# The 42-column remainder of a feed-forward: from half-array tiles to the full shape of TensorE

## The chip, the cores and the metric

The kernel runs on one core of a Trainium2 chip (trn2). The metric is the device time of one execution in microseconds (us); lower is better. The times shown are those of several executions of the same program, and one further execution was recorded by the hardware profiler.

## The reference

The program computes `x = x + ffn(cond(x, t))` for 32 sequences of 256 tokens with 256 channels, in float32. `cond` is a gated scan over the tokens (512 inner channels, a state of 16). `ffn` has two layers; each is a windowed attention with 8 heads and then a gated feed-forward. Only the feed-forward is touched here:

```python
HID = int(DIM * 4 * 2 / 3)          # 682
...
h = shift_token(x)
mu = h.mean(-1, keepdims=True)
var = h.var(-1, keepdims=True)
h = (h - mu) / jnp.sqrt(var + 1e-05) * lg + lb
h = h @ w1 + b1                     # 256 -> 2 x 682
a, g = jnp.split(h, 2, axis=-1)
h = a * jax.nn.gelu(g, approximate=False)
x = x + h @ w2 + b2                 # 682 -> 256
```

682 is five blocks of 128 and a remainder of 42 (`MREM`). The last of the six blocks is what this case is about.

## The kernel before

**Tiling and order.** The 32 sequences go through the scan in four groups of eight (`GB`). The scan of group g+1 runs beside attention and feed-forward of group g; the feed-forward of the last group runs with no scan beside it. For attention and feed-forward the unit of work is one sequence in one layer, of which there are 32 x 2 = 64. Each unit has a list of stages, eight to a step (`ST = 8`), written out by hand in `attend`, `feed` and `fetch`; at every stage a share of the scan's steps is put out as well (`scan_to`). The instructions of each engine run in the order in which the program puts them out. Matrix products are in float32, and each appears in the trace as two matmul records with their two weight loads (two passes).

**The feed-forward of a unit.** `normalise`, `apply` and `spread` make `self.h`, the normalised channels-by-tokens block (2 x 128 channels by 256 tokens). `widen(m)` (L1313, matmuls at L1326) multiplies it with block m of `w1`, once for the linear half `pa` and once for the gate half `pg`, each over two blocks of channels (`KM = 2`); ScalarE then writes Gelu(pg + bias) to a tile `ag` (L1334). `product(m)` (L1337, instruction at L1342) multiplies `ag` by `pa` + bias on VectorE. `narrow(d)` (L1348, matmuls at L1354), for each of the two output halves d, sums over the six blocks `ag[m]` with `w2` into `po_f`, and VectorE adds the residual (L1365). In `feed`, for unit n, `widen(m)` stands at stage 4 + m and `product(m)` at stage 5 + m of step n+2, and `narrow(d)` at stage 3 + d of step n+3. A remainder's `widen(5)` is therefore at stage 1 of step n+3.

**The remainder as it is now.** In `widen`, the linear half (42 columns) goes to partitions 0 to 41 of a PSUM bank and the gate half (42 columns) to partitions 64 to 105. These are two tiles of the array, 64 columns wide, and the loop alternates between them. `product` writes its result twice, to partitions 64 to 105 and 0 to 41 of `ag`. `narrow` uses the lower copy for d = 0 and the upper one for d = 1, each as a matmul over 42 rows, in a tile of 64 rows. The 42 rows of `w2` for the upper copy are loaded by an extra transfer (L954) to partitions 64 on.

**Buffers.** `ag` has seven buffers and takes six of them for each unit. All PSUM tiles share one ring of eight banks (`ps_w`). Weights are single buffers, reloaded for each group and layer by SyncE's queue (`load_weights`, L939). In memory, `w2` is padded with zero rows to 6 x 128; `w1` is not padded, its 1364 columns are the linear half and then the gate half.

Of the kernel before, what the change touches and what calls it, by code (L numbers as in the profile page):

```python
# [10 lines left out]
FP = mybir.dt.float32  # L11
# [3 lines left out]
ALU = mybir.AluOpType  # L15
# [4 lines left out]
P = 128  # L20
S = 256
DM = 256
KM = DM // P
# [14 lines left out]
DH = 64  # L38
W = 128
NW = S // W  # L40
HID = 682
MCH = [(o, min(P, HID - o)) for o in range(0, HID, P)]
MREM = MCH[-1][1]
# [30 lines left out]
def kernel(  # L74
# [29 lines left out]
    nc = tc.nc  # L104
# [58 lines left out]
    for j in range(NJ):  # L163
# [18 lines left out]
        out=mask_t[:, 0:W], in_=mask_t[:, 0:W], compare_op=ALU.is_ge, fill=MASKED_LOW,  # L182
# [3 lines left out]
        out=mask_t[:, W : 2 * W], in_=mask_t[:, W : 2 * W], compare_op=ALU.is_ge,  # L186
# [22 lines left out]
    b1_sb = const.tile([P, L, 2, len(MCH)], FP, tag="b1_sb", name="b1_sb")  # L209
# [7 lines left out]
    for i in range(2):  # L217
        t = const.tile([P, NI * (P + GB)], FP, tag=f"ly{i}", name=f"ly{i}")
# [3 lines left out]
    def program(ctx, exact):  # L222
        rpool = ctx.enter_context(tc.tile_pool(name="res", bufs=1, reuse_waits="tile"))
# [7 lines left out]
        aw = ctx.enter_context(tc.tile_pool(name="aw", bufs=3, reuse_waits="tile"))  # L231
        ps_w = ctx.enter_context(tc.tile_pool(name="psw", bufs=8, space=PSUM, reuse_waits="tile"))

        def bank(pool, tag, name):
            return pool.tile([P, DI], FP, tag=tag, name=name)
# [694 lines left out]

        ys, res, wt, projected = {}, {}, {}, {}

        def load_res(g, b):
            t = rpool.tile([P, KM, 1 + S], FP, tag=f"res{b}", name=f"res{b}")
            nc.gpsimd.memset(t[:, :, 0:1], 0.0)
            nc.sync.dma_start(out=t[:, :, 1:], in_=ys[g][:, :, b, :])
            res[b] = t

        def load_weights(l, kind, i=0):  # L939
            shape, srcs = {  # L940
                "qkv": lambda: ([P, KM, DI], [wqkv[:, l, :, i * DI : (i + 1) * DI]]),
                "wo": lambda: ([P, NC_, DM], [wo[:, l]]),
                "w1": lambda: (
                    [P, KM, 2, MCH[i][1]],
                    [w1[:, l, :, x * HID + MCH[i][0] :][:, :, 0 : MCH[i][1]] for x in range(2)],
                ),
                "w2": lambda: ([P, len(MCH), DM], [w2[:, l]]),
            }[kind]()
            t = wpool.tile(shape, FP, tag=f"{kind}{i}", name=f"{kind}{i}")
            for x, src in enumerate(srcs):  # L950
                nc.sync.dma_start(out=t[:, :, x] if len(srcs) > 1 else t, in_=src)
            if kind == "w2":
                last = len(MCH) - 1
                nc.sync.dma_start(out=t[DH : DH + MREM, last], in_=w2[0:MREM, l, last])  # L954
            wt[kind, i] = t

        WEIGHTS = [("qkv", 2), ("qkv", 0), ("qkv", 1), ("wo", 0)]
# [67 lines left out]
        if exact:  # L1025
# [4 lines left out]
                out=mask[:, 0:W], in_=mask[:, 0:W], compare_op=ALU.is_ge, fill=MASKED,  # L1030
# [3 lines left out]
                out=mask[:, W : 2 * W], in_=mask[:, W : 2 * W], compare_op=ALU.is_ge, fill=MASKED,  # L1034
# [218 lines left out]
        class FeedForward:  # L1253
# [59 lines left out]
            def widen(self, m):  # L1313

                l, n = self.l, MCH[m][1]
                ps = bank(ps_w, "w", "pa")
                pa = ps[0:n, 0:S]
                if n == P:
                    pg, b1g = ps[:, S:], b1_sb[:, l, 1, m : m + 1]
                    order = [(x, k) for x in (1, 0) for k in range(KM)]  # L1320
                else:

                    pg, b1g = ps[DH : DH + n, 0:S], b1g_sb[DH : DH + n, l : l + 1]
                    order = [(x, k) for k in range(KM) for x in (1, 0)]
                for x, k in order:
                    nc.tensor.matmul(  # L1326
                        pg if x else pa,
                        wt["w1", m][:, k, x],
                        self.h[:, k],
                        start=(k == 0),  # L1330
                        stop=(k == KM - 1),
                    )
                ag = aw.tile([P, S], FP, tag="ag", name="ag", bufs=7)
                nc.scalar.activation(ag[0:n], pg, AF.Gelu, bias=b1g)  # L1334
                self.pa[m] = pa, ag

            def product(self, m):  # L1337
                l, n = self.l, MCH[m][1]
                pa, ag = self.pa.pop(m)

                for r in (0,) if n == P else (DH, 0):
                    nc.vector.scalar_tensor_tensor(  # L1342
                        ag[r : r + n], pa, b1_sb[0:n, l, 0, m : m + 1], ag[0:n],
                        ALU.add, ALU.mult,
                    )
                self.ag[m] = ag

            def narrow(self, d):  # L1348
                if d == 0:
                    self.po = bank(ps_w, "w", "po_f").rearrange("p (d t) -> p d t", d=KM)  # L1350
                for m, (_, n) in enumerate(MCH):

                    r0 = 0 if n == P else d * DH
                    nc.tensor.matmul(  # L1354
                        self.po[:, d],
                        wt["w2", 0][r0 : r0 + n, m, d * P : (d + 1) * P],
                        self.ag[m][r0 : r0 + n],
                        start=(m == 0),
                        stop=(m == len(MCH) - 1),
                    )  # L1360
                l, last = self.l, self.l == L - 1
                if d == 0 and last:
                    self.fo = ap_.tile([P, KM, S], FP, tag="swp", name="fo", bufs=3)
                rv = res[self.b][:, d, 1:]
                nc.vector.scalar_tensor_tensor(  # L1365
                    self.fo[:, d] if last else rv,
                    self.po[:, d], b2_sb[:, l, d : d + 1], rv, ALU.add, ALU.add,
                )
                if last and d == KM - 1:
                    b = self.g * GB + self.b  # L1370
                    xs = ap_.tile([P, KM, S], FP, tag="rot", name="xs", bufs=4)
                    nc.sync.dma_start(out=xs, in_=xT[:, :, b, :])
                    nc.gpsimd.tensor_add(self.fo, self.fo, xs)
                    nc.sync.dma_start(out=outT[:, :, b, :], in_=self.fo)

        NM = len(MCH)
        if exact:
            for g in range(NG):
                for _ in scan_slots([g]):
                    pass  # L1380
                for b in range(GB):
                    load_res(g, b)
                for l in range(L):
                    for kind, i in WEIGHTS:
                        load_weights(l, kind, i)
                    for _ in attention(l):
                        pass
                    for b in range(GB):
                        ff = FeedForward(g, l, b)
                        ff.normalise()  # L1390
                        ff.apply()
                        ff.spread()
                        for m in range(NM):
                            ff.widen(m)
                            ff.product(m)
                        for d in range(KM):
                            ff.narrow(d)
            return
# [43 lines left out]
        def fetch(n, g, l, b):  # L1442

            if b == GB - 1 and (g, l) != (NG - 1, L - 1):
                nl = (l + 1) % L
                for i, a in ((5, 2), (6, 0), (6, 1)):
                    stage(n - 1, i, load_weights, nl, "qkv", a)
                stage(n + 2, 0, load_weights, nl, "wo")
                for m in range(NM):
                    stage(n + 2, 6 + m, load_weights, nl, "w1", m)  # L1450
                stage(n + 3, 6, load_weights, nl, "w2")
            if l == L - 1 and g < NG - 1:
                stage(n + 6, 2, load_res, g + 1, b)
# [22 lines left out]
        for b in range(GB):  # L1476
            load_res(0, b)
# [7 lines left out]
        for t in range(max(stages) + 1):  # L1485
# [3 lines left out]
            g, r = divmod(t + 1 + group - reload, group)  # L1489
# [10 lines left out]
    with tc.If(fits > 0) as which:  # L1500
        with ExitStack() as es:
            program(es, False)
    with which.Else():
        with ExitStack() as es:
            program(es, True)
# [108 lines left out]
```

## Time and profile before

| what | value |
|---|---|
| median of 3 runs | 3692.19 us (3688.66 to 3693.34) |
| span of the profiled execution (first to last instruction; the profile gives no other time for it) | 3693.9 us |
| mean granted TensorE clock | 0.988 |
| busy TensorE / its weight loads | 3580.5 / 2234.3 us |
| busy VectorE / ScalarE / GpSimd | 2714.2 / 2163.0 / 1812.1 us |
| matmul records at L1326 (`widen`) / L1354 (`narrow`) | 3072 / 1536 |
| instructions at L1342 (`product`) | 448, of which 128 on 42 partitions, 475 ns each |

How to read the lines that follow: in the tables of groups, a line gives the line of the code, the engine (PE is TensorE, PEld its weight loads, DVE VectorE, ACT ScalarE, POOL GpSimd, SP SyncE), the operation, output<-inputs, for matmuls rows*columns of the stationary block and the moving operand, the count, and then busy time, mean duration and idle time before it. A line of the timeline gives the start in us, the time from there to the end of the last instruction merged into it, and the instructions. The ends of matmuls are modelled, and the records of consecutive matmuls overlap; their starts are what to compare. A line of the waits gives who waited for whom, us in total, times and the longest.

### The profile page before, as it was taken

Reading aid. Unit: us, or ns where it says so; the run is one execution under the profiler, and the core shown is the slowest. Engines: PE = TensorE matmul, PEld = TensorE weight load, DVE = VectorE, ACT = ScalarE, POOL = GpSimd, SP = SyncE. Lnnn points to the kernel's source line nnn. Section 1 sums busy time; section 2 is a strip of 40 time slices with the busy share of each in tenths; the row PEclk is TensorE's granted clock in tenths of the full one; section 3 lists DMA queues with packets and bytes.
Section 4 is the critical chain, followed back from the end, with each engine's and each line's share of the span. In section 5 each row is a group of like instructions: output and inputs, shape, how many; then the busy total and the mean of one; then the engine's idle time right before and its main releaser. Section 6 shows DMA issues by size and latency. Waiting matters only on the chain.

```text
span 3693.9 us, 56916 instructions
## 1 busy us (share of the span) xinstructions
PE 3580.5 (97%) x19804; PEld 2234.3 (60%) x19804; DVE 2714.2 (73%) x5177; ACT 2163.0 (59%) x3689; POOL 1812.1 (49%) x1745
## 2 busy tenths in 40 slices
PE   7999989999999999999999999999999999999999
PEld 4444335666566566666666666666666666666666
DVE  5888889878787777877787778877777445455553
ACT  3666656666666666666666666666666444444442
POOL 4433366445455455545455556544554444444551
PEclk9999999999999999999999999999999999999999
DMA  7877655544454555444454555544453212011101
GB/s 196 209 201 206 185 164 148 134 110 135 124 139 119 140 141 145 131 112 124 119 138 124 135 145 138 134 111 130 111 134 114 59 35 59 12 30 39 30 27 36
DMA packets 469213, 435.80 MB, mean 118 GB/s; under 512 B 228835, under 2 KB 308532, under 8 KB 468788
## 3 DMA queue, kind: packets, MB, share of 16 engines
q1 hardware_dynamic: 384466, 420.05, 42.2%
q10 hardware_dynamic: 84450, 12.01, 2.1%
q8 instruction: 160, 2.62, 0.3%
q14 instruction: 137, 1.12, 0.1%
HBM read 383.70 MB, written 46.66 MB: 117 GB/s over the span
## 4 chain that ended last, share of the span: by engine, by line
PE 67%; DVE 15%; DMA 5%; POOL 5%; ACT 3%; issue 3%; SPq 0%; ACTq 0%; DVEq 0%; POOLq 0%
PE ps_qkv L965 13%; PE pa L1326 13%; PE po_f L1354 8%; DVE h L706 6%; PE y L718 5%; PE ps_wo L1015 4%; PE sc L1174 4%; DMA xrep<-xnd 4%; PE ov L1223 3%; PE ps_out L796 3%; PE ps_in L398 2%; PE tr_qk L1004 2%; DVE acc L488 2%; PE rs L1204 2%; ACT xrep L696 2%
## 5 line engine op out<-in xcount | busy, mean ns | idle before, releaser
L706 DVE CUSTOM_DVE_ANT_0 h<-h,xrep,lim 128x512 f32<-128x512 f32 x1024 | 947.3, 925 | 232.2 <-ACT xrep L696 197.5
L696 ACT ACTIVATE xrep<-xrep,beta 128x512 f32<-128x512 f32 x960 | 672.8, 719 | 336.1 <-DMA xrep<-xnd 239.0
L965 PE MATMUL ps_qkv<-qkv,res 128*128 128x512 f32 x1536 | 724.7, 607 | 19.2 <-DVE ag L1342 8.3
L1326 PE MATMUL pa<-hT,w 128*128 128x256 f32 (+1 forms) x3072 | 690.4, 387 | 1.6 <-ACT hT L1305 1.3
L1326 PEld LDWEIGHTS pa<-hT,w 128*128 128x128 f32 (+1 forms) x3072 | 493.8, 178 | 186.6 <-issue 77.8
L989 POOL TENSOR_TENSOR rot<-rot,swp 128x512 f32<-128x512 f32 x256 | 335.4, 1310 | 482.4 <-DVE swp L986 353.2
L965 PEld LDWEIGHTS ps_qkv<-qkv,res 128*128 128x128 f32 x1536 | 278.0, 191 | 328.9 <-issue 250.0
L997 POOL TENSOR_TENSOR rn<-ss,neg_half 128x8 f32<-128x8 f32 x256 | 459.2, 1794 | 15.6 <-DVE ss L995 5.4
L1354 PE MATMUL po_f<-ag,w 128*128 128x256 f32 (+1 forms) x1536 | 388.5, 394 | 11.5 <-DVE ag L1342 7.6
L1342 DVE SCALAR_TENSOR_TENSOR ag<-pa,b_sb,ag 128x256 f32<-128x256 f32 (+1 forms) x448 | 213.1, 476 | 234.4 <-ACT ag L1334 231.8
L718 PE MATMUL y<-h,ly 128*32 128x512 f32 x2048 | 357.1, 614 | 10.7 <-DVE h L706 7.9
L1279 POOL TENSOR_TENSOR rstd<-ve,neg_half 128x2 f32<-128x2 f32 x64 | 46.4, 724 | 614.8 <-DVE ve L1277 596.9
L1354 PEld LDWEIGHTS po_f<-ag,w 128*128 128x128 f32 (+1 forms) x1536 | 273.4, 189 | 119.5 <-issue 47.3
L998 POOL TENSOR_TENSOR rot<-rot,rn 128x512 f32<-128x512 f32 x256 | 291.0, 1137 | 20.1
L978 ACT ACTIVATE sq<-ps_qkv 128x512 f32<-128x512 f32 x256 | 151.9, 596 | 229.3 <-PE ps_qkv L965 181.0
L1334 ACT ACTIVATE ag<-pa,b_sb 128x256 f32<-128x256 f32 x320 | 150.4, 470 | 206.1 <-PE pa L1326 203.6
L488 DVE SCALAR_TENSOR_TENSOR acc<-xr,wc_sb,acc 128x256 f32<-128x256 f32 x384 | 192.7, 524 | 55.7 <-POOL acc L477 55.1
L1015 PE MATMUL ps_wo<-oT,wo 128*128 128x256 f32 x1024 | 231.7, 379 | 0.3 <-ACT ag L1334 0.2
L981 DVE TENSOR_TENSOR rot<-ps_qkv,rc_sb 128x512 f32<-128x512 f32 x256 | 174.8, 683 | 73.4 <-ACT sq L978 72.3
L1174 PE MATMUL sc<-qT,kT 64*128 64x128 f32 (+1 forms) x2048 | 221.3, 345 | 0.0
L1183 ACT ACTIVATE pT<-sc 128x512 f32<-128x512 f32 x384 | 208.6, 596 | 15.2 <-PE sc L1174 13.2
L1015 PEld LDWEIGHTS ps_wo<-oT,wo 128*128 128x128 f32 x1024 | 194.3, 190 | 28.2 <-ACT ag L1334 1.0
(153 smaller groups left out, 5493.7 us busy)
## 6 DMA issues: line engine op xcount, KB each, us to landing
xrep<-xnd SPq DMA_DIRECT2D x960, 256.0 KB
rb<-inv SPq DMA_DIRECT2D x128, 256.0 KB
xnd<-xn SPq DMA_DIRECT2D x64, 256.0 KB
qkv<-in_wqkv_dram SPq DMA_DIRECT2D x24, 512.0 KB
ahead<-xs_a SPq DMA_DIRECT2D x48, 256.0 KB
xp<-ahead SPq DMA_DIRECT2D x48, 256.0 KB
xd<-xnd SPq DMA_DIRECT2D x192, 64.0 KB
w<-in_w_dram SPq DMA_DIRECT2D x80, 128.0 KB
```

Source lines behind the costliest of these rows:

```text
L488: nc.vector.scalar_tensor_tensor(acc, xr[:, :, k : k + CH], wc_sb[:, ch, k : k + 1], acc, ALU.mult, ALU.add,)
L696: scaled = nc.scalar.activation(bx, ck[c].pop(("bx", t), bx), AF.Copy, scale=ck[c]["beta"][:, t : t + 1])
L706: nc.vector._custom_dve(TENSOR_ADD_SAT, out=h_new, in0=state["h"], in1=bx, s0=ck[c]["lim"][:, 0, t : t + 1], s1=ck[c]["lim"][:, 1, t : t + 1],
L718: nc.tensor.matmul(ck[c]["y", hb][32 * q : 32 * q + 32, :], ly[hb % 2][:, 32 * t : 32 * t + 32], ck[c].pop(("h", hb * TB + t)), start=(i = ...
L965: nc.tensor.matmul(ps, res[b][:, k, t0 : t0 + W], wt["qkv", a][:, k], start=(k == 0), stop=(k == KM - 1),)
L989: nc.gpsimd.tensor_add(rot, rot, swp)
L997: nc.gpsimd.tensor_tensor(rn, ss, neg_half, ALU.pow)
L998: nc.gpsimd.tensor_mul(rot, rot, bc(rn, 2, DH))
L1015: nc.tensor.matmul(po[:, d], wt["wo", 0][:, c, d * P : (d + 1) * P], oT[:, c, :], start=(c == 0), stop=(c == NC_ - 1),)
L1174: nc.tensor.matmul(banks[r][:, i, :], kT[rows, i0 + i, kw * W : (kw + 1) * W], qT[rows, i0 + i, kw * W :], start=self.apart, stop=self.apa ...
L1326: nc.tensor.matmul(pg if x else pa, wt["w1", m][:, k, x], self.h[:, k], start=(k == 0), stop=(k == KM - 1),)
L1354: nc.tensor.matmul(self.po[:, d], wt["w2", 0][r0 : r0 + n, m, d * P : (d + 1) * P], self.ag[m][r0 : r0 + n], start=(m == 0), stop=(m == le ...
```

## The change

The two halves of the remainder become one stationary block of 106 columns: 64 columns that begin with the 42 linear ones (the other 22 are the first columns of the gate half of `w1`, whose results are not read), and then the 42 gate columns. One chain of two matmuls takes the place of two chains; the results lie on the same partitions as before. The remainder's `ag` becomes a tile of its own, `ag_rem`, allocated once and set to zero once by GpSimd; Gelu and product write its first 42 partitions, product only once. `narrow` runs over all 128 rows for every block: rows 42 to 127 are zero in `ag_rem` and in `w2`. The extra transfer for `w2` goes, the first half of the remainder's `w1` transfer has 64 columns and not 42, and `ag` has six buffers.

```diff
+        ag_rem = rpool.tile([P, S], FP, tag="ag_rem", name="ag_rem")
+        nc.gpsimd.memset(ag_rem, 0.0)
...
                 "w1": lambda: (
-                    [P, KM, 2, MCH[i][1]],
-                    [w1[:, l, :, x * HID + MCH[i][0] :][:, :, 0 : MCH[i][1]] for x in range(2)],
+                    [P, KM, 2, P] if MCH[i][1] == P else [P, KM, 1, DH + MREM],
+                    [w1[:, l, :, x * HID + MCH[i][0] :] for x in range(2)],
                 ),
...
-            for x, src in enumerate(srcs):
-                nc.sync.dma_start(out=t[:, :, x] if len(srcs) > 1 else t, in_=src)
-            if kind == "w2":
-                last = len(MCH) - 1
-                nc.sync.dma_start(out=t[DH : DH + MREM, last], in_=w2[0:MREM, l, last])
+            if kind == "w1":
+
+                dst = [t[:, :, 0], t[:, :, 1]] if MCH[i][1] == P else [
+                    t[:, :, 0, 0:DH], t[:, :, 0, DH:]
+                ]
+            else:
+                dst = [t]
+            for out, src in zip(dst, srcs):
+                nc.sync.dma_start(out=out, in_=src[:, :, 0 : out.shape[-1]])
...
                 if n == P:
                     pg, b1g = ps[:, S:], b1_sb[:, l, 1, m : m + 1]
-                    order = [(x, k) for x in (1, 0) for k in range(KM)]
+                    dst, xs = (pa, pg), (1, 0)
                 else:
 
                     pg, b1g = ps[DH : DH + n, 0:S], b1g_sb[DH : DH + n, l : l + 1]
-                    order = [(x, k) for k in range(KM) for x in (1, 0)]
-                for x, k in order:
-                    nc.tensor.matmul(
-                        pg if x else pa,
-                        wt["w1", m][:, k, x],
-                        self.h[:, k],
-                        start=(k == 0),
-                        stop=(k == KM - 1),
-                    )
-                ag = aw.tile([P, S], FP, tag="ag", name="ag", bufs=7)
+                    dst, xs = (ps[0 : DH + n, 0:S],), (0,)
+                for x in xs:
+                    for k in range(KM):
+                        nc.tensor.matmul(
+                            dst[x],
+                            wt["w1", m][:, k, x],
+                            self.h[:, k],
+                            start=(k == 0),
+                            stop=(k == KM - 1),
+                        )
+                if n == P:
+                    ag = aw.tile([P, S], FP, tag="ag", name="ag", bufs=6)
+                else:
+                    ag = ag_rem
                 nc.scalar.activation(ag[0:n], pg, AF.Gelu, bias=b1g)
...
-                for r in (0,) if n == P else (DH, 0):
-                    nc.vector.scalar_tensor_tensor(
-                        ag[r : r + n], pa, b1_sb[0:n, l, 0, m : m + 1], ag[0:n],
-                        ALU.add, ALU.mult,
-                    )
+                nc.vector.scalar_tensor_tensor(
+                    ag[0:n], pa, b1_sb[0:n, l, 0, m : m + 1], ag[0:n], ALU.add, ALU.mult
+                )
...
-                for m, (_, n) in enumerate(MCH):
-
-                    r0 = 0 if n == P else d * DH
+                for m in range(len(MCH)):
                     nc.tensor.matmul(
                         self.po[:, d],
-                        wt["w2", 0][r0 : r0 + n, m, d * P : (d + 1) * P],
-                        self.ag[m][r0 : r0 + n],
+                        wt["w2", 0][:, m, d * P : (d + 1) * P],
+                        self.ag[m],
```

## The prediction

> **What bounds the kernel now.** I first read the busy shares: TensorE 97%, VectorE 73%. A busy TensorE is not proof, because the recorded matmuls overlap (each lasts longer than the distance to the next). So I asked for TensorE's waits in the stretch in which the last group's scan is over, and for the busy times by stretch (columns PE, PEld, DVE, ACT, POOL, each with its count):
>
> ```profile
> PE 3580.5 (97%) x19804; PEld 2234.3 (60%) x19804; DVE 2714.2 (73%) x5177; ACT 2163.0 (59%) x3689; POOL 1812.1 (49%) x1745
> ...
> PE po_f L1354 <- DVE fo L1365: 0.6, 1, 0.6
> ...
> 1000.00:1600.00 600.00, 585.56 (x3349) 370.16 (x3349) 471.65 (x886) 377.06 (x647) 314.33 (x300) 0.99 0.51 134
> 1600.00:2800.00 1200.00, 1188.64 (x6902) 753.41 (x6901) 951.52 (x1810) 765.46 (x1305) 619.22 (x578) 1.00 0.49 128
> 2800.00:3694.00 894.00, 886.10 (x5102) 603.48 (x5101) 460.05 (x913) 415.80 (x659) 394.22 (x314) 1.00 0.15 41
> ```
>
> From 2800 us to the end the second line is all that TensorE waited: 0.6 us of 894. From 1600 to 2800 its waits add up to 10.8 us of 1200 (9.0 of it for a product, DVE L1342), from 620 to 1000 to 12.6 us of 380. So the kernel runs at the pace at which TensorE starts matmuls, with VectorE next: 79% busy from 1600 to 2800, 84% from 620 to 1000, 51% at the end. What counts is the distance between matmul starts. I read it from the timeline of TensorE and of its weight loads, cut so narrowly that single instructions show:
>
> ```profile
> 3224.85 1.92 PEld L1354 LDWEIGHTS po_f<-ag,w 128*128 128x128 f32 x9 [0.24 <-issue]
> 3227.10 0.29 PEld L1354 LDWEIGHTS po_f<-ag,w 42*128 42x128 f32 x2 [0.33 <-issue]
> ```
>
> The same on TensorE itself, around the 42-row block of narrow and then around the 42-column block of widen:
>
> ```profile
> 3226.80 0.38 PE L1354 MATMUL po_f<-ag,w 128*128 128x256 f32 x1
> 3227.10 0.48 PE L1354 MATMUL po_f<-ag,w 42*128 42x256 f32 x1
> 3227.42 0.38 PE L1354 MATMUL po_f<-ag,w 42*128 42x256 f32 x1
> 3227.73 0.48 PE L1326 MATMUL pa<-hT,w 128*128 128x256 f32 x1
> 3228.05 0.38 PE L1326 MATMUL pa<-hT,w 128*128 128x256 f32 x1
> ...
> 3212.16 0.59 PE L965 MATMUL ps_qkv<-qkv,res 128*128 128x512 f32 x1
> 3212.68 0.42 PE L1326 MATMUL pa<-hT,w 128*42 128x256 f32 x2
> 3213.68 0.70 PE L965 MATMUL ps_qkv<-qkv,res 128*128 128x512 f32 x1
> 3214.21 0.59 PE L965 MATMUL ps_qkv<-qkv,res 128*128 128x512 f32 x1
> ```
>
> And its weight loads in a run of 512-column passes:
>
> ```profile
> 3214.64 0.19 PEld L965 LDWEIGHTS ps_qkv<-qkv,res 128*128 128x128 f32 x1 [0.24 <-issue]
> 3215.07 0.19 PEld L965 LDWEIGHTS ps_qkv<-qkv,res 128*128 128x128 f32 x1 [0.24 <-issue]
> ```
>
> One matmul of the program stands as two records (two passes): L1326 has 3072 records = 64 sequences x layers x (5 x 4 + 4) x 2. In full shape a pass of 256 columns starts every (1.92 - 0.19) / 8 = 0.216 us (first line), one of 512 columns every 0.43 us (last fence). Around the 42-row block the distances are 0.30, 0.32, 0.31 and 0.32 us: entering it, inside it, leaving it, and the first pass after it.
>
> **What the Trainium skill says.** "TensorEngine Tiling (Array Packing)", Key Properties: "Changing tiling mode (not just tile) drains the TensorE". The trace agrees: the weight loads stand idle 0.33 us on both sides of the block against 0.03 inside a run. "TensorE: Matmul & The Clock Gate", Part 3, says that matmuls in different column tiles run at the same time, some 4 ns apart. The trace agrees: the x2 at 3212.68 is a pair that starts inside 0.01 us, and eight 42-column records last from 3212.68 to 3213.68, four slots and not eight. The same page under LDWEIGHTS: the load's time goes by columns, not rows. The trace agrees: 42 rows x 128 columns 186 ns, 128 x 128 190, 128 x 42 117.
>
> **The change, part by part** (per sequence and layer; there are 64).
>
> Widen remainder: 8 records in 4 paired slots become 4 records of 106 columns. The slots are as many, so only the mode changes count. Now: 3212.16 to 3214.21 = 2.05 us. In full shape: 0.43 + 4 x 0.216 + 0.43 = 1.72. Gain 0.33. A 106-column load is not in the trace; between 117 and 190 ns, it stays under the 0.216 of a pass and is hidden either way.
>
> Narrow remainder: still 2 records for each half d, now over 128 rows. For d = 1: 3226.80 to 3228.05 = 1.25 us now, 4 x 0.216 = 0.86 in full shape, gain 0.39. For d = 0 the next work is a turn of 128 columns (starts every 0.11 us): from 3220.45 to 3221.55 = 1.10 now, 3 x 0.216 + 0.11 = 0.76 then, gain 0.34.
>
> Sum: 0.33 + 0.39 + 0.34 = **1.06 us**, all on the engine that sets the pace; x 64 = 68 us. Four of the 64 widen blocks come behind y (a 32-column tile), whose drain stays: they keep some 0.2 us each, 1 us in all.
>
> VectorE: the second product on the remainder goes, 64 x 0.475 us (42x256 row of L1342) = 30 us of its 2714. It lies beside TensorE's work, so I count it at nothing; in the middle stretches it offsets half of the extra share that VectorE gets as the same work is squeezed into less time. Up to the 10.8 us of TensorE's waits there could go with it; the ones I looked at end on 128-row products, so I take 0.
>
> Buffers: ag_rem is one buffer, ag has six. The Gelu that writes ag_rem must wait until the sequence before has been narrowed (d = 1). That Gelu waits in any case for its own widen matmuls, which TensorE executes after those narrow matmuls: five stages of the schedule after narrow d = 1 of the sequence before. The same holds for ag: buffer 5i + m was last read by that narrow. So no new wait for Gelu, nor for anything queued behind it on ScalarE. Cost 0, both bounds.
>
> The rest: a 128x256 memset on GpSimd (0.32 us by the row of sel, L161) goes ahead of the scan, where GpSimd sits idle for 8 us from 5.4 us on: 0 to 0.3 us, I take 0. On SP's queue 8 issues of 42 KB fall away (0.35 us each), and 8 first halves grow from 42 to 64 columns; they run layers ahead of use, 0 either way.
>
> How much of the 68 arrives depends on who is close behind. Narrow records per stretch / 24 give the sequences:
> 620 to 1000: 6.5 x 1.06 = 6.9; VectorE 84%, waits 3.3%: I keep half, 3.5.
> 1000 to 1600: 11 x 1.06 = 11.7; waits 14 us of 600: I keep 0.8, 9.3.
> 1600 to 2800: 23.5 x 1.06 = 24.9; waits 0.9%: I keep 0.9, 22.4.
> From 2800: 23 x 1.06 = 24.4; nothing else near: all.
> Sum 59.6, less the 1 us above: **some 59 us**. The shares kept are my choice; the bounds are none and all. The profiled span, 3693.9, is 1.7 us above the median of the runs, so 3693.9 - 59 = 3634.9 for a profile and **3633** for the median.
>
> **Rivals.**
> *All of it, and more* (chance 0.10): the middle keeps everything and the shorter VectorE queue also removes waits: 67 + 8 = 75, 3617.
> *The scan becomes the bound in the middle* (0.10): the chain of steps (DVE h L706, 10% of the chain of waits before 1000 us) has no slack. For it: VectorE's 79 to 84%, and xrep transfers in the chain. Against: h L706 sat idle 232 us, mostly for xrep. Then the last group gains, and three tenths of the rest (43.5): 24 + 13 = 37, 3655.
> *106 columns are not the full shape* (0.10): the block still drains on both sides, and no second tile shares its slots. Then widen takes as long as now (four slots, two drains), narrow alone gains 0.73 x 64 x 0.88 = 41: 3651. For it: 106 is no multiple of 32. Against: 42 columns already run.
> *Slower* (0.03): the 106 columns are carried out as two parts, 64 and then 42, each pass drained alone. From eight starts at 0.21 us, (0.73 + 1.00) / 8, narrow's gain is eaten; at the 0.32 seen inside a drained block it is 8 x 0.32 = 2.56 against 1.00, a loss of 1.56 - 0.73 = 0.83 x 64 = 53 us: 3745. Nothing in the trace shows such a split.
> The likeliest case, 3622 to 3645, has 0.67.
>
> **How the numbers follow.** Time 3633. The likeliest case and the neighbours at 3651 and 3655 (in part) give 8 in 10: 3619 to 3654. A difference of 0.2% (7.4 us) is about what a measurement of this kernel can tell from none. Every case but the slower one gains well over that; 0.02 I leave for an end between: faster 0.95, same 0.02, slower 0.03.
>
> **What would show each step.** Right: widen's records fall from 3072 to 2816, product's from 448 to 384; starts 0.216 us apart through the 106-column and the last narrow passes; the last group's period from one narrow to the next goes from 40.3 to 39.2 us. Wrong: a 0.3 us start at the 106-column block (rival three), or, with starts as said, TensorE's waits between 620 and 2800 up by over 20 us (rival two). The forecast itself falls if the last group gains less than 20 us.

## The result, and the profile after

| what | before | after |
|---|---|---|
| median of 4 runs each, one chip | 3691.48 us | 3636.0 us |
| range of these runs | 3688.66 to 3693.34 | 3633.24 to 3639.81 |
| span of the profiled execution | 3693.9 us | 3631.4 us |

The ratio is 0.9848, with a 95% interval of 0.9836 to 0.986: 55 us faster by the medians, 62.5 by the two profiled executions. The forecast was 3633 us, between 3619 and 3654. A span is shorter than the time of the same execution: the profiled execution after has a span of 3631.4 us and a time of 3633.24, which is the fastest of its four. With the same difference, the one before would have a time of some 3695.7 us (an estimate), above the slowest of its four. So this pair of profiles overstates the gain; the medians are the better measure of the sum, and the profiles show where it comes from.

The busy shares, then TensorE's waits from 2800 us to the end, then the busy times from 1600 to 2800 us (the length, then PE, PEld, DVE, ACT, POOL, then the granted clock, the DMA share and GB/s):

```profile
PE 3511.0 (97%) x19548; PEld 2271.0 (63%) x19548; DVE 2684.7 (74%) x5113; ACT 2160.2 (59%) x3689; POOL 1816.2 (50%) x1746
```

```profile
PE po_f L1362 <- DVE fo L1373: 0.6, 1, 0.6
```

```profile
1600.00:2800.00 1200.00, 1181.40 (x6892) 778.44 (x6889) 941.86 (x1785) 773.87 (x1321) 616.65 (x569) 1.00 0.49 129
```

TensorE lost 256 records (19804 to 19548), VectorE 64 instructions and 30 us (2714.2 to 2684.7). TensorE's share is 97% as before: the share does not show the gain. In the last stretch it still waits 0.6 us in all. From 1600 to 2800 its busy time fell from 1188.6 to 1181.4 of 1200, so there it stands still more than it did.

The starts around the two blocks, from the timeline of TensorE in cuts so narrow that one or two instructions show, widen's block first and narrow's for d = 1 second:

```profile
3163.34 0.59 PE L973 MATMUL ps_qkv<-qkv,res 128*128 128x512 f32 x1
3163.77 0.59 PE L1335 MATMUL pa<-hT,w 128*106 128x256 f32 x2
3164.20 0.59 PE L1335 MATMUL pa<-hT,w 128*106 128x256 f32 x2
3164.63 0.59 PE L973 MATMUL ps_qkv<-qkv,res 128*128 128x512 f32 x1
3165.06 0.59 PE L973 MATMUL ps_qkv<-qkv,res 128*128 128x512 f32 x1
...
3177.30 0.38 PE L1362 MATMUL po_f<-ag,w 128*128 128x256 f32 x1
3177.52 0.38 PE L1362 MATMUL po_f<-ag_rem,w 128*128 128x256 f32 x1
3177.73 0.38 PE L1362 MATMUL po_f<-ag_rem,w 128*128 128x256 f32 x1
3177.95 0.38 PE L1335 MATMUL pa<-hT,w 128*128 128x256 f32 x1
3178.16 0.38 PE L1335 MATMUL pa<-hT,w 128*128 128x256 f32 x1
```

Widen's block: 3163.34 to 3165.06 is 1.72 us, for 2.05 before; four passes 0.215 us apart, and the distances on either side are no longer than those in a run. Narrow's: 3177.30 to 3178.16 is 0.86 us, for 1.25. The weight loads show the same:

```profile
3171.30 0.41 PEld L1362 LDWEIGHTS po_f<-ag_rem,w 128*128 128x128 f32 x2
3177.30 0.41 PEld L1362 LDWEIGHTS po_f<-ag_rem,w 128*128 128x128 f32 x2
...
L1335 PEld LDWEIGHTS pa<-hT,w 128*106 128x106 f32 x256 | 43.3, 172 | 29.0 <-issue 17.4 <-ACT oT L1238 1.4 <-DVE xr L471 0.8
```

No idle time is put down in front of narrow's last two loads, where 0.33 us stood. The last line is from the table of groups: a load of 106 columns takes 172 ns, inside the bounds of 117 and 190.

### The profile page after: what moved, and what is told of

Its sections match the earlier page's. It is cut to its first block, busy times and chain, and to the rows that moved or that the text cites. A ratio compares the mean times of both kernels' runs of the same rounds, so it can differ in the third digit from the quotient of the medians.

```text
span 3631.4 us, 56312 instructions
## 1 busy us (share of the span) xinstructions
PE 3511.0 (97%) x19548; PEld 2271.0 (63%) x19548; DVE 2684.7 (74%) x5113; ACT 2160.2 (59%) x3689; POOL 1816.2 (50%) x1746
## 4 chain that ended last, share of the span: by engine, by line
PE 62%; DVE 18%; DMA 7%; POOL 6%; ACT 4%; issue 3%; SPq 0%; ACTq 0%; DVEq 0%; POOLq 0%
PE ps_qkv L973 13%; PE pa L1335 12%; DVE h L706 7%; PE po_f L1362 7%; PE y L718 4%; DMA xrep<-xnd 4%; PE ps_wo L1023 4%; PE sc L1182 4%; PE ov L1231 3%; DVE acc L488 2%; PE ps_out L796 2%; PE tr_qk L1012 2%; PE ps_in L398 2%; ACT xrep L696 2%; PE rs L1212 2%
## 5 line engine op out<-in xcount | busy, mean ns | idle before, releaser
L973 PE MATMUL ps_qkv<-qkv,res 128*128 128x512 f32 x1536 | 715.0, 600 | 21.0 <-DVE ag L1353 9.7
L1335 PE MATMUL pa<-hT,w 128*128 128x256 f32 (+1 forms) x2816 | 679.9, 383 | 1.6 <-ACT hT L1313 0.9
L1335 PEld LDWEIGHTS pa<-hT,w 128*128 128x128 f32 (+1 forms) x2816 | 514.9, 188 | 147.5 <-issue 55.7
L1362 PE MATMUL po_f<-ag,w 128*128 128x256 f32 x1280 | 307.4, 387 | 5.1 <-DVE fo L1373 5.1
L1006 POOL TENSOR_TENSOR rot<-rot,rn 128x512 f32<-128x512 f32 x256 | 292.4, 1142 | 20.1
L1353 DVE SCALAR_TENSOR_TENSOR ag<-pa,b_sb,ag 128x256 f32<-128x256 f32 x320 | 152.7, 477 | 197.7 <-ACT ag L1346 197.3
L1362 PEld LDWEIGHTS po_f<-ag,w 128*128 128x128 f32 x1280 | 236.1, 191 | 69.4 <-issue 11.9
```

Of the source, the lines that this page charges most:

```text
L973: nc.tensor.matmul(ps, res[b][:, k, t0 : t0 + W], wt["qkv", a][:, k], start=(k == 0), stop=(k == KM - 1),)
L1006: nc.gpsimd.tensor_mul(rot, rot, bc(rn, 2, DH))
L1335: nc.tensor.matmul(dst[x], wt["w1", m][:, k, x], self.h[:, k], start=(k == 0), stop=(k == KM - 1),)
L1362: nc.tensor.matmul(self.po[:, d], wt["w2", 0][:, m, d * P : (d + 1) * P], self.ag[m], start=(m == 0), stop=(m == len(MCH) - 1),)
```

## The experiments

Three theories went in. **Theory 1**: what goes is the extra distance between TensorE's starts when it enters and leaves another tile shape. **Theory 2**: VectorE's second product carries a large part. **Theory 3**: both matmul blocks give equal parts. All ratios are to the kernel before, run in turn on the same chip. A "visit" below is a stay of TensorE in another tile shape, with its entry and its exit.

Two quantities are read off each trace, from the starts of the first matmul of narrow for d = 0, once per unit (the 64 units counted from 0). "Last group" is the distance from unit 50 to 51, where no scan runs; there every unit takes the same time. "Middle" is the distance from unit 18 to 41 over 23; before it runs from 1642.17 to 2842.16 us. How far such a figure scatters: the change and e9, whose programs are the same there, agree in the middle within 0.01 us; the change and e8 part by 0.06.

| run | ratio (95% interval) | last group, us per unit | middle, us per unit |
|---|---|---|---|
| before | 1 | 40.32 | 52.17 |
| the change | 0.9848 (0.9836 to 0.986) | 39.25 | 51.54 |
| e1 narrow only | 0.9892 (0.9877 to 0.9906) | 39.58 | 51.67 |
| e2 widen only | 0.9962 (0.9949 to 0.9975) | 39.99 | 51.97 |
| e3 change, second product | 0.9864 (0.9849 to 0.9879) | 39.25 | 51.57 |
| e4 before, one product | 0.9986 (0.9976 to 0.9996) | 40.32 | 52.12 |
| e5 before, fewer taps | 0.9863 (0.9848 to 0.9878) | 40.32 | 51.62 |
| e6 change, fewer taps | 0.9704 (0.9691 to 0.9718) | 39.25 | 50.76 |
| e7 before, halves in turn | 1.0002 (0.9993 to 1.0012) | 40.33 | 52.17 |
| e8 change, 128 columns | 0.9837 (0.9823 to 0.985) | 39.25 | 51.48 |
| e9 change, scores in a row | 0.9815 (0.9802 to 0.9828) | 38.46 | 51.54 |
| e10 before, one tile | 1.0099 (1.0084 to 1.0115) | 41.17 | 52.70 |

**e1, narrow alone.** Over the kernel before:

```diff
-                ag = aw.tile([P, S], FP, tag="ag", name="ag", bufs=7)
+                if n == P:
+                    ag = aw.tile([P, S], FP, tag="ag", name="ag", bufs=6)
+                else:
+                    ag = ag_rem
...
-                for r in (0,) if n == P else (DH, 0):
...
-                    r0 = 0 if n == P else d * DH
...
+                        wt["w2", 0][:, m, d * P : (d + 1) * P],
+                        self.ag[m],
```

> Narrow alone in full shape (ag_rem, one product), widen as before in two 42-column tiles. Theory 1, the distances between TensorE's starts around a change of tile shape: narrow's two blocks give 0.73 us for each of 64 units, 47 us in all, of which some 41 arrive: ratio to before about 0.989. Theory 2, the second product on VectorE is a large part of the gain: this kernel drops that product too, so it gets nearly the whole gain of the change, 55 us, ratio 0.985. Theory 3, half and half between the two matmul blocks: 28 us, 0.9925.

Measured: 3650.46 us, 0.9892. In the last group a unit takes 40.32 - 39.58 = 0.74 us less; theory 1 had 0.73. The ratios of theories 2 and 3 lie outside the interval.

**e2, widen alone.** Over the changed kernel, `ag`, product and narrow are put back:

```diff
+                for r in (0,) if n == P else (DH, 0):
+                    nc.vector.scalar_tensor_tensor(ag[r : r + n], pa, ..., ag[0:n], ...)
...
+                    r0 = 0 if n == P else d * DH
```

> Widen alone with one block of 106 columns; the product is written twice and narrow works on 42 rows as before. Theory 1: 0.33 us for each of 64 units, 21 us, some 17 arrive: ratio about 0.995, and eight 42-column records in 1.00 us become four 106-column ones 0.216 us apart with no 0.3 us start before or after. Theory 2: the product is still there twice, so little is gained, under 5 us, 0.999 or more. That 106 columns are not the full shape: 0 us as well, but with a 0.3 us start at the block.

Measured: 3674.84 us, 0.9962. In the last group 40.32 - 39.99 = 0.33 us per unit, as worked out. The two parts add up: (1 - 0.9892) + (1 - 0.9962) = 0.0146, and the whole change gives 0.0152.

**e3, the second product put back** into the changed kernel, on rows where `w2` is zero:

```diff
-                nc.vector.scalar_tensor_tensor(ag[0:n], pa, ..., ag[0:n], ALU.add, ALU.mult)
+                for r in (0,) if n == P else (DH, 0):
+                    nc.vector.scalar_tensor_tensor(ag[r : r + n], pa, ..., ag[0:n], ...)
```

> The changed kernel with the second product put back: VectorE writes the remainder's product also to partitions 64 to 105 of ag_rem, where w2 has zero rows, so the sum is the same. 64 x 0.475 = 30 us more work on VectorE, TensorE's work unchanged. Theory 1: the last group shows no change, the rest at most a few us: ratio to before 0.985 to 0.987. Theory 2: 10 to 15 us are lost, ratio 0.988 to 0.990.

**e4, one product in the kernel before**. Both halves of narrow then read the lower copy, and the extra transfer for `w2` goes too:

```diff
-                for r in (0,) if n == P else (DH, 0):
+                nc.vector.scalar_tensor_tensor(ag[0:n], pa, ..., ag[0:n], ALU.add, ALU.mult)
...
-                    r0 = 0 if n == P else d * DH
+                    r0 = 0
```

> The kernel before with one product only: both halves of narrow read partitions 0 to 41, so all tiles of TensorE stay as they were (42 columns, 42 rows), and the extra transfer of w2 is gone. VectorE loses 30 us of work. Theory 1: within 5 us of before, ratio 0.9985 to 1.000. Theory 2: 10 to 15 us faster, ratio 0.996 to 0.997.

Measured: e3 0.9864, e4 0.9986; the last group does not move in either (39.25, 40.32). So the second product is no large part, and theory 2 falls. That e4's last group does not move also shows that reading one 64-row tile twice, and not two tiles in turn, changes nothing there. The product is not free, though: e4's interval excludes 1, at 0.0014 or 5 us (the extra transfer is in that too); e3's ratio lies 0.0016 above that of the change, which the overlapping intervals leave unproven. Both profiles put it in the same place, between units 0 and 18: there e4 takes 962.8 us for 970.7 before, and e3 957.1 for 949.0 in the change, 8 us each. The change, e8 and e9 agree within 0.5 us in that stretch (949.0, 949.2, 948.7), but before and e7 part by 4 (970.7, 966.5), so e3's 8 us is the safer of the two. The middle moves by 0.05 and 0.03 us per unit.

**e5 and e6, less work on VectorE**, in the kernel before and in the changed one alike. Both leave out two of the three later taps of the convolution, so they do not compute the layer:

```diff
-                for k in range(1, TAPS):
+                for k in range(1, 2):
```

> The kernel before with two of the three later taps of the convolution left out (L487 runs over one tap): 256 of 384 instructions of 0.52 us, 134 us less on VectorE, all beside the scan; nothing changes on TensorE. A base for the next run. If TensorE's starts set the time, this alone gains what TensorE waited for VectorE in the middle, at most 25 us: ratio 0.993 to 0.999. If VectorE set it in the middle, half of the 134 us or more: 0.98 or less.

> The changed kernel with the same two taps left out. If the part of the gain that is missing in the middle (from 1600 to 2800 us some 0.6 us per unit arrived of 1.06) is lost to waits for VectorE's products, then with VectorE lighter it arrives: 62 to 68 us against the run of the kernel before with the same two taps left out, ratio between the two 0.982, and some 1.0 us per unit in the middle. If it is lost to something else (transfers, ScalarE), the difference stays at 55 us, ratio between the two 0.985, and 0.6 us per unit.

Measured: e5 3639.54 us, e6 3580.46. The e5 ratio lies between the two cases that I had set out. By its trace, 20.1 of 54.4 us are gained before the first narrow (at 651.4 us for 671.5), and I had counted waits of TensorE only after that. But TensorE's order was not left alone there, as I had expected it to be: up to 553 us its instructions stand in another order in e5 in many places. How much of the 20.1 us is the lighter VectorE and how much the order stays open. The kernels with all taps spread from 662.8 to 673.1 us at that point.

From unit 18 to 41 the order is the same in all four kernels, and there they can be compared. The middle gains 51.62 - 50.76 = 0.86 us per unit from e5 to e6, for 52.17 - 51.54 = 0.63 with all taps. By the medians the gain is 59.1 us, between the two cases that I had set out, and its ratio, 0.9704 / 0.9863 = 0.984, cannot be told from 0.9848. TensorE's waits in the middle, first before and after with all taps, then e5 and e6:

```profile
PE ps_qkv L965 <- DVE ag L1342: 5.7, 8, 1.2
PE sc L1167 <- DVE ag L1342: 2.6, 4, 0.8
PE ps_qkv L965 <- DVE rinv L1212: 1.0, 2, 0.8
PE ps_qkv L965 <- DVE swp L986: 0.8, 1, 0.8
...
PE ps_qkv L973 <- DVE ag L1353: 6.8, 8, 0.9
PE sc L1175 <- DVE ag L1353: 6.0, 6, 1.3
PE ps_qkv L973 <- DVE rinv L1220: 1.8, 4, 0.6
PE ps_wo L1023 <- ACT ag L1346: 1.2, 1, 1.2
PE ps_qkv L973 <- DVE swp L994: 0.6, 1, 0.6
```

```profile
PE ps_qkv L965 <- DVE ag L1342: 1.6, 3, 0.9
...
PE ps_qkv L973 <- DVE ag L1353: 3.7, 5, 0.9
PE ps_qkv L973 <- DVE swp L994: 0.6, 1, 0.6
```

The waits for `ag` are waits for a PSUM bank: neither a qkv nor a score block reads `ag`, but it wants a bank of the ring that still holds a `pa`, whose product stands in VectorE's queue. One case: near 2000 us in the changed kernel Gelu is done at 1994.2 us, VectorE works off the scan's convolution and other steps until it starts the product at 1999.99, and TensorE, ready to go on with the scores, stands for 1.3 us.

From before to after, all waits in this stretch grew by 6.3 us (10.1 to 16.4); with VectorE lighter they grew by 2.7 (1.6 to 4.3). So VectorE takes back part of the gain, and with less work it takes back less: 0.23 us per unit of the 1.06 - 0.63 = 0.43 that are missing. The traces also show that hardly anything is missing at the blocks themselves. Over the 23 units the starts around narrow's and widen's blocks close up by 23.0 us in all, of 24.4 worked out; 8.4 us are lost again at other instructions of TensorE, the largest part at the mask matmuls of the scores (L1167, then L1175), from which to the next block TensorE takes 44.1 us in sum, for 39.6.

**e7, the halves in turn**, in the kernel before:

```diff
-                    order = [(x, k) for k in range(KM) for x in (1, 0)]
+                    order = [(x, k) for x in (1, 0) for k in range(KM)]
```

> The kernel before, with the remainder's two 42-column halves one after the other (all gate matmuls, then all linear ones) and no longer alternating. What it tells apart: whether the alternating halves ran side by side. If so, the eight records now take up to eight slots of 0.216 us: 1.73 us for 1.00 us, up to 0.73 x 64 = 47 us slower, ratio up to 1.012; with one pair overlapping where the halves meet, 40 us. If the 64-column tiles gave no overlap, no change.

Measured: 3688.64 us, 1.0002. My reading of the alternation was wrong. The timeline of TensorE before and then in e7:

```profile
3212.68 1.06 PE L1326 MATMUL pa<-hT,w 128*42 128x256 f32 x8
3213.68 3.70 PE L965 MATMUL ps_qkv<-qkv,res 128*128 128x512 f32 x8
...
3206.95 1.07 PE L1326 MATMUL pa<-hT,w 128*42 128x256 f32 x8
3207.95 1.12 PE L965 MATMUL ps_qkv<-qkv,res 128*128 128x512 f32 x2
```

The eight records still take 1.00 us, although the four of the gate half stand ahead of the four of the linear half in the program. The order in the queue did change, as far as the trace can tell: the two starts of a pair lie 13 to 15 ns apart in e7 in all units, and 5 to 8 ns before. Either there is no overlap by tile at all, or TensorE brings the second tile's matmuls forward. e10 tells these apart.

**e10, both halves in one tile**, in the kernel before:

```diff
-                    pg, b1g = ps[DH : DH + n, 0:S], b1g_sb[DH : DH + n, l : l + 1]
-                    order = [(x, k) for k in range(KM) for x in (1, 0)]
+                    pg, b1g = ps[0:n, S:], b1_sb[0:n, l, 1, m : m + 1]
+                    order = [(x, k) for x in (1, 0) for k in range(KM)]
```

> The kernel before, with the remainder's gate half on partitions 0 to 41 as well, in the other half of its PSUM bank, so that both 42-column halves use the same 64-column tile, one after the other; Gelu reads it there, the rest as before. The run with the halves in turn showed that their order alone leaves the eight records side by side in 1.00 us. If it is the two tiles that let them run side by side, whatever their order, then in one tile they take eight slots: 1.73 us, 0.73 us more for each of 64 units, some 42 of 47 us arrive: ratio to before 1.011. If the halves overlapped for another reason: no change, 1.000.

Measured: 3725.17 us, 1.0099. Its timeline:

```profile
3226.80 1.92 PE L1326 MATMUL pa<-hT,w 128*42 128x256 f32 x8
3228.66 3.70 PE L965 MATMUL ps_qkv<-qkv,res 128*128 128x512 f32 x8
```

1.86 us for the same eight records in the same order: two tiles are what lets them run side by side. The surplus is 0.86 us, four slots of 0.216 us, and not the 0.73 that I expected: there I had set eight clean slots against 1.00 us, which holds four slots and the cost of entering and leaving. In the last group it arrives whole (41.17 - 40.32 = 0.85).

**e8, the block padded to 128 columns**:

```diff
-                    [P, KM, 2, P] if MCH[i][1] == P else [P, KM, 1, DH + MREM],
+                    [P, KM, 2, P] if MCH[i][1] == P else [P, KM, 1, P],
...
-                    dst, xs = (ps[0 : DH + n, 0:S],), (0,)
+                    dst, xs = (ps[:, 0:S],), (0,)
```

> The changed kernel with the block padded from 106 to 128 columns by 22 further columns of w1, whose results are not read. What it tells apart: whether the width 106 costs anything against a whole block. If every width over 64 is the full shape: no change from the changed kernel, ratio to before 0.983 to 0.987. If 106 still carries part of a switch: faster than the changed kernel by up to 0.3 us per unit, 20 us, ratio 0.980.

An extra transfer fills the 22 columns. Measured: 3630.2 us, 0.9837, with 39.25 us per unit in the last group as in the change. There the width 106 costs nothing against 128.

**e9, a version that the result points to.** If a visit of another shape costs 0.35 us or more, visits that can be joined should be. Over the changed kernel, in the last group alone:

```diff
-            stage(n, 3, at.scores, b, 0, 0, 2)
             stage(n, 2, at.scores, b, 1, 0, HEADS // 2)
-            stage(n, 5, at.scores, b, 0, 2, 2)
+            stage(n, 2 if at.apart else 3, at.scores, b, 0, 0, 2)
+            stage(n, 2 if at.apart else 5, at.scores, b, 0, 2, 2)
```

> The changed kernel, and in the last group the three blocks of attention scores (64-row tiles) of a unit put out one after the other in one stage, where they stood in three: two stays in the 64-row shape fewer for each of 16 units. Theory 1 (each stay costs its entry, its first pass, its exit and the next first pass, 0.35 to 0.39 us as at narrow): 32 x 0.37 = 12 us less than the changed kernel, ratio to before about 0.981. Rival: six of the ring's eight PSUM banks now wait for ScalarE's Exp at once, and TensorE stands for 1 us or more per unit: 0.985 to 0.99, with waits for pT in the last group.

Measured: 3622.0 us, 0.9815, the fastest version here that computes the whole layer; its interval ends below where that of the change begins. First the weight loads of the three blocks in the change, then the timeline of TensorE in e9 and its waits after 2800 us:

```profile
3168.15 0.97 PEld L1182 LDWEIGHTS sc<-qT,kT 64*128 64x128 f32 x16 [0.76 <-issue]
3172.47 0.73 PEld L1182 LDWEIGHTS sc<-qT,kT 64*128 64x128 f32 x8 [0.17 <-issue]
3184.93 0.73 PEld L1182 LDWEIGHTS sc<-qT,kT 64*128 64x128 f32 x8 [0.33 <-issue]
...
3200.84 2.89 PE L1182 MATMUL sc<-qT,kT 64*128 64x128 f32 x32
3203.66 0.48 PE L1362 MATMUL po_f<-ag,w 128*128 128x256 f32 x1
```

```profile
PE po_f L1362 <- DVE fo L1373: 0.6, 1, 0.6
```

All 32 records stand in one run, no new wait appears, and a unit takes 39.25 - 38.46 = 0.79 us less: 0.39 for each of the two visits saved. The rival, a stall on PSUM banks, did not come.

## Why the prediction was right, point by point

**The sum per unit** (0.33 + 0.39 + 0.34 = 1.06 us) was right: the last group's unit went from 40.32 to 39.25 us, 1.07, where I had named 40.3 to 39.2, and e1 and e2 give its parts separately, 0.74 and 0.33. The records fell to 2816 at widen and the products to 384 as said. From unit 41 to unit 63, the last, the two traces part by another 22.5 us; I had 24.4 for one unit more.

**The shares kept** were the chosen part, and one of them failed: "1600 to 2800 ... I keep 0.9, 22.4". In the middle 0.63 of 1.06 us arrived, a share of 0.6, and 14.6 us in all. It is no accident of one trace: e1 kept 0.50 of 0.74, e2 0.20 of 0.33, and e10, which adds work, passed on only 0.53 of its 0.85. TensorE's waits of 0.9% were read as how far the next engine is behind. They say only that TensorE seldom stands now; VectorE at 79% busy, with products and scan steps in one queue, was close enough to take back some four tenths of each of these shifts. The waits moved with them: 10.1 us before, 16.4 in the change, and 4.2 in e10. This resembles rival two, but it is not what that rival said. There the scan's own chain of steps had no slack and set the pace; here products that stand behind scan steps hold PSUM banks. By the sign that I had set for it, over 20 us more of waits between 620 and 2800 us, rival two did not come: they went from 37.6 to 43.0.

**The second product at nothing** was low: some 5 us by e4, between units 0 and 18.

**620 to 1600** was near, once the product is taken out: I kept 12.8 us; from unit 0 to unit 18 the profiles part by 970.7 - 949.0 = 21.7, of which some 8 are the product (e3, e4) and 13.7 are left. e7, whose median is that of before, takes 4.2 us less there than the profile of before, so some 4 us of this are not settled.

One cause of such a difference is visible: the order of an engine's instructions is not quite what the description of the kernel says. TensorE's is the same in both traces but for one place, near 990 us, where before the matmuls of narrow's remainder (d = 0) stand behind the first transposition of `tp_hn` and wait for a product:

```profile
997.50 0.79 PE L1354 MATMUL po_f<-ag,w 42*128 42x256 f32 x1 [5.23 <-DVE ag L1342]
```

In the change this wait is 2.3 us. Of the kernels that write the product twice, before, e2, e3 and e7 have this order and a wait of 5.0 to 5.6 us, e5 and e10 have not; those that write it once never have it. So about 3 of the product's 8 us stand at this one place, and how much of them is VectorE's load and how much the order is open. VectorE's order differs in more places, from 780 us on.

So the total, 59 forecast and 55 measured, came out close partly by luck: the middle's 8 us too many met the product's 5 and what is unsettled in the early stretch. The 62.5 us of the two profiles are 3.2 before the first narrow, where the change has nothing to act on, then 21.7, 14.6 and 22.5, and 0.5 at the end. The forecast from TensorE alone stands on the last group, where it is exact. That the forecast mixed a span with a time (3693.9 against the median) does not touch it: 59 us under the median is 3633 as well.

**The other rivals.** "All of it, and more" failed in the middle. 106 columns are the full shape (no long start at the block, and e8). The slower case, two parts for each pass, did not occur. The Gelu that writes `ag` and `ag_rem` waited for its own matmuls alone, as said, but for 0.6 us once, so six buffers and one cost nothing there; ScalarE appears in TensorE's waits of the middle with 1.2 us, once.

## What to carry to other kernels

Where TensorE sets the pace, count visits of other tile shapes, not only matmuls: in this kernel a visit of a 42-row or 64-row block cost 0.34 to 0.39 us beyond its passes. So a remainder of few passes that is short of rows or columns was cheaper here as a full block with zeros, and blocks of one odd shape were cheaper side by side in the program (e9). Tiles that run side by side pay for their entry and exit only if they save enough slots; the two 42-column halves saved as many slots as one joint block does, and paid 0.33 us on top. Waits of 0.9% did not measure slack here: ask how busy the next engine is and what it holds meanwhile, and test the share that arrives with a change of known size in both directions, as e1 and e10 do here.

## What the runs showed of the hardware that I had not expected

Matmuls of two column tiles ran side by side although four records of one tile stood ahead of those of the other in the program: 1.00 us for eight records in either order, 1.86 us in one tile (e7, e10). The Trainium skill, "TensorE: Matmul & The Clock Gate", Part 3, has them start strictly in program order; here the measurement differs. The records do not name the tile, so a single start cannot be assigned; but eight starts in four close pairs within 1.00 us do not go together with two runs of four, one after the other.
